# Strassen units of a fused FFN kernel in another order, with loads and sums at other places

## The chip, the cores and the metric

The kernel runs on one NeuronCore of a Trainium2 chip. The metric is the device time of one execution in microseconds; the median of several runs counts. One execution was also taken with the hardware profiler, and everything said of the inside of the kernel comes from that trace.

## The reference

Four layers are added to x (32 sequences, 64 channels, length 1024), each as a residual:

```python
x = x + s4_convolution(x, log_dt, C, log_A_real, A_imag, D, length)   # FFT convolution along L, masked
x = x + einsum('bsi,boi->bso', x, w1[ids1])                           # per-sequence 1024x1024 matrix
x = x + einsum('bij,bkj->bik', x, w2[ids2])                           # another one
gate = x @ W_gate.T + 0.5 * lora(x, A_gate, B_gate)                   # hidden size F = 2752, rank 16
up   = x @ W_up.T   + 0.5 * lora(x, A_up, B_up)
act  = silu(gate) * up
x = x + act @ W_down.T + 0.5 * lora(act, A_down, B_down)
```

All of it is fp32.

## The kernel before, in words

**Chunks.** The 32 sequences are cut into four chunks `c` of eight, so that a chunk has 512 columns. The convolution (L1037 on) runs first, for all sequences; chunk 0's result stays in SBUF, the results of chunks 1 to 3 go to the DRAM tensor `cd`. Then come chunk 0's 16 adapters (two layers of eight sequences, `adapter`, L287): each streams eight weight tiles of 512 KB through 128 matmul records into one PSUM bank `pa`. After that the feed-forward part `ffn` runs for chunk after chunk, and the 16 adapters of chunk c+1 are spread over the feed-forward part of chunk c as they come out of the generator `others`; `other(us)` (L851) first lets VectorE do postponed sums (`fill(us)`) and then runs one adapter.

**Blocks.** The hidden rows come in ten pairs, two pairs to a group `gi` (0 to 4), in three blocks: group 0; groups 1 and 2; groups 3 and 4. Of each group `gated` (L699) computes gate, then up. After a block, its part of the down product is added to x (`po<-act,wd` in the profile, 28 to 64 matmul records for each of four row blocks `h`). Rows that do not fit the Strassen scheme (`rest`, L730) are computed after block 0 with plain matmuls (`pr`); they are called the rest rows below.

**Strassen.** In chunk 0 gate and up use one level of the Winograd form of Strassen's scheme (`halves`), and the sums of weights are stored for later chunks on the way: `kept(q)` makes sums of sums and stores them in the DRAM tensors `sums` through two rotating buffers, `kept_parts` stores `parts`. Chunks 1 to 3 use two levels (`quarters`, L584): seven outer products, numbered 0 to 6 in the code and p1 to p7 as results, each made of the seven inner products P1 to P7 of `product(bank, i, start)`. One call of `quarters` makes gate or up of one group in 196 matmul records; there are 30 calls. Outer products are made one or two at a time by `unit(js, ...)`: before in the order (0), (5, 6), (4, 3), (1, 2). A unit with two has products of eight matmul records, a unit with one has products of four.

**Inside a unit.** Four PSUM banks `pa` to `pd` are used: P1 and P2 in `pa`, P6 in `pb`, P7 and then P4 in `pc`, P5 and then P3 in `pd`. ScalarE copies P1 and P6 out; VectorE makes u = P1 + P6 (L647), c22 = P7 + u (L649), c22 += P5 (L651), c21 = `pc` + u (L659), c12 = `pd` + u (L661). P4 is added by TensorE onto P7 in `pc`, and so has to wait until VectorE has read `pc` at L649; P3 is added onto P5 in `pd` and waits for L651.

**Order of the work.** TensorE, VectorE and ScalarE run in the order in which the code is written. The queues of SyncE (SP) and GpSimd (POOL) are ordered by the scheduler of the tile framework, and an SP load that waits for a buffer or a tile holds up those behind it. All weight tiles, `wa`, `wb`, `wd`, `wf`, `wr` and the convolution results `cv`, share a pool of nine buffers of 512 KB. Sums on VectorE that can wait are put into the deque `later` with an estimated cost each; `fill(us)` takes from its front while the estimates fit into `us`, `flush()` takes all.

**Places that the change touches.** `bring(c, quarters)` (L230) asks for x of the next chunk and for quarters of the convolution results, `take` (L246) puts the eight sums x += cv (two for each quarter) into `later`. Both are called by `between(i)` (L856), i = 2 gi after gate and 2 gi + 1 after up: quarters 0 and 1 after group 0's gate, 2 and 3 after block 0's first step of the rest rows. x has two buffers, so the request for the next x waits until the last chunk's rows in that buffer have been stored (`store`, L840). `between` runs no adapter for i = 2, `flush()` and one adapter for i = 3, and one adapter for i over 3; after the last group of blocks 1 and 2 there are a `flush()` and another adapter. `down_sides` (L879) loads and sums one tile of down weights; for the first tile of a block it is called through `behind`, after the last sum of up. `moving_act` makes the four sums of moving sides for one row pair of a group's activations, `times_up` the product of gate and up. `moving_of` makes the sides of the next chunk's x in four steps during the last down block.

Of the kernel before, what the change touches and what calls it, by code (L numbers as in the profile page):

```python
# [39 lines left out]
TH = TC // 2  # L40
# [33 lines left out]
def kernel(  # L74
# [25 lines left out]
    nc = tc.nc  # L100
# [27 lines left out]
    xs = [x_tile(0)]  # L128
# [101 lines left out]
    def bring(c, quarters):  # L230

        if quarters[0] == 0:
            xs.append(x_tile(c))
            with tc.issue_after(done_first[0]):
                nc.sync.dma_start(xs[c], xt[:, c])
        n = H // HA // 4
        for q in quarters:
# [8 lines left out]
    def take(c, quarters):  # L246
        n, half = H // 4, KT * BC // 2
        for q in quarters:
            t = came.pop(q)
            for i in (0, 1):  # L250

                def add(q=q, t=t, i=i):
                    rows_ = slice(i * half, (i + 1) * half)
                    xv = xs[c].rearrange("p k (b h) -> p (k b) h", h=H)
                    xv = xv[:, rows_, q * n : (q + 1) * n]
                    nc.vector.tensor_add(xv, xv, t.rearrange("p i k -> p k i")[:, rows_])

                later.append((1.0, add))
# [233 lines left out]
    def halves(c, gi, g, o, xb, sides0, behind, also=lambda: None):  # L492
# [37 lines left out]
        for m in range(MG):  # L530
# [27 lines left out]
            if m == 0:  # L558
                copy_lt()
                for at_, x in zip((wts, sts, sides_of), halves_sides(gi, g, 1)):  # L560
                    at_.append(x)
                kept_parts()
                also()
            else:
                fill(1.3)
            product(pc, 6, True)
            nc.vector.tensor_add(c22, pc, u)
            if m == 1:
                fill(1.3)
            product(pb, 4, True)  # L570
            nc.vector.tensor_add(c22, pb, c22)
            kept(2 * m)
# [4 lines left out]
            kept(2 * m + 1)  # L577
# [6 lines left out]
    def quarters(c, gi, g, o, xb, _, behind, also=lambda: None):  # L584
# [26 lines left out]
        def unit(js, start, mid, copies=None):  # L611
# [28 lines left out]
            fill(start)  # L640
# [8 lines left out]
            nc.vector.tensor_add(c22, pc, u)  # L649
            product(pd, 4, True)  # L650
            nc.vector.tensor_add(c22, pd, c22)  # L651
            if callable(mid):
                mid()
            else:
                fill(mid)
            product(pa, 1, False)
            nc.scalar.copy(c11, pa)
            product(pc, 3, False)
            nc.vector.tensor_add(c21, pc, u)  # L659
# [18 lines left out]
        (p1,) = unit((0,), 0.9, 0.0, copy_lt)  # L678
        nc.scalar.copy(c12, p1)
        also()  # L680
        add(c11, p1, l11)
        p6, p7 = unit((5, 6), 1.3, 1.3)
        add(c12, c12, p6)
        add(c21, c12, p7)

        def l12_():
            add(c12, c12, l12)
            fill(0.6)

        p5, p4 = unit((4, 3), 0.5, l12_)  # L690
        add(c22, c21, p5)
        add(c21, c21, p4)
        add(c12, c12, p5)
        p2, p3 = unit((1, 2), 0.0, lambda: add(o[:, 1], o[:, 1], lt[:, 1]))
        add(c11, c11, p2)
        add(c12, c12, p3)
        return behind()

    def gated(c, gi, xb, sides0, between, behind):  # L699


        f = quarters if c else halves
        act = apool.tile([P, 2, MG, TC], F32, tag="act", name=f"act_{c}_{gi}")
        sides0 = f(c, gi, 0, act, xb, sides0, lambda: c or halves_sides(gi, 1, 0))
# [14 lines left out]
        def moving_act(m):  # L719
            a = act[:, :, m]  # L720
            q = [a[:, h, t * TH : (t + 1) * TH] for h in (0, 1) for t in (0, 1)]
            ab.append(moving(*q, *(act_d[:, m, j] for j in range(4))))
# [3 lines left out]
        for m in range(MG):  # L726
            later.append((1.7, lambda m=m: moving_act(m)))
# [65 lines left out]
    def moving_of(c):  # L793
# [25 lines left out]
        def halves_of(i):  # L819
            b11, b12, b21, b22 = (q_of(k, t)[i] for k in (0, 1) for t in (0, 1))  # L820
            moving(b11, b12, b21, b22, *(at_(j)[i] for j in (4, 5, 6, 3)))
            for j, q in zip(range(3), (b11, b21, b22)):
# [6 lines left out]
            lambda: halves_of(1),  # L829
            lambda: (  # L830
                nc.vector.tensor_sub(t1, b12, b11),
# [14 lines left out]
    def ffn(c, xb, sides0, others):  # L846
# [24 lines left out]
        for block, (m0, m1) in enumerate(BLOCKS):  # L871
# [24 lines left out]
            for gi in groups:  # L896
                end = gi == groups[-1]

                def behind():
                    if end:  # L900
                        down_sides()
                    elif c == 0:
                        return halves_sides(gi + 1, 0, 0)

# [31 lines left out]
            if last:  # L936
# [3 lines left out]
                for t in (0, 1):  # L940
                    wl_t = wl[:, t].rearrange("p i f -> p (i f)")
                    gather(wl_t[FIRST], bd, rows_half[FIRST, c, t : t + 1])
                    with tc.issue_after(done_first[0]):
                        nc.sync.dma_start(wl_t[SECOND], wd_rest)
# [5 lines left out]
            for h in range(KH):  # L950
# [7 lines left out]
                for s0 in range(m0, m1, SEG):  # L958
# [6 lines left out]
                    elif end and last:  # L965
                        if h == 0:
                            nc.vector.tensor_sub(wl[:, 1, 0], wl[:, 1, 0], wl[:, 1, 1])
# [524 lines left out]
```

## Time and profile before

| what | us |
|---|---|
| runs before (three) | 2430.5, 2431.6, 2436.9 |
| median | 2431.6 |
| the profiled execution: time | 2439.8 |
| the profiled execution: span | 2438.2 |
| mean granted TensorE clock in it | 0.987 |
| DMA moved | 686 MB, mean 281 GB/s |

The span is the time from the first to the last instruction of the program in the profile, and the execution's time is 1.6 us more. PE is TensorE's matmuls, PEld its weight loads, DVE VectorE, ACT ScalarE, POOL GpSimd, SP SyncE, whose DMA issues are marked SPq. In a line of the page's list of groups, the first pair of numbers after the bar is the busy time of the group and the mean length of one instruction in ns, and what follows the second bar is the idle time of the engine before these instructions and what ended it. An fp32 matmul appears as two records.

### The profile page before, as it was taken

What the parts mean: (1) busy time and instruction counts of PE and PEld (TensorE: products, weight loads), DVE (VectorE), ACT (ScalarE), POOL (GpSimd) and SP (SyncE); (2) the same over time, 40 slices, a digit from 0 to 9 for tenths busy, and PEclk for the clock granted to TensorE, in tenths of its full rate; (3) what the DMA queues carried; (4) which work ended last, traced back from release to release, by engine and by line L of the source; (5) the groups of instructions that cost most, each with busy time, mean ns of one, the idle gap of its engine ahead of it and who ended that gap; (6) DMA issues with size and microseconds to landing.
All of it is one profiled execution on the core that took longest, in us unless ns stands there. A gap on an engine that the chain in (4) does not pass through costs nothing.

```text
span 2438.2 us, 53622 instructions
## 1 busy us (share of the span) xinstructions
PE 2293.7 (94%) x21674; PEld 1875.5 (77%) x21674; DVE 1321.0 (54%) x2762; ACT 386.6 (16%) x848; POOL 267.6 (11%) x387
## 2 busy tenths in 40 slices
PE   5999889999999898999999998999999899999998
PEld 4986447876667678798688688797688678798987
DVE  7411128775357555666345555666345556566574
ACT  4200012111001112131012112121012112121220
POOL 4322011211011210000000110100000110100000
PEclk9999999999999999999999999999999999999999
DMA  8999998489989856489989957489989957375581
GB/s 299 348 322 370 407 376 291 177 316 345 329 295 338 317 216 250 154 299 342 349 306 345 335 211 260 142 304 339 346 309 337 332 214 247 114 257 200 199 279 40
DMA packets 202121, 686.00 MB, mean 281 GB/s; under 512 B 26242, under 2 KB 28546, under 8 KB 201362
## 3 DMA queue, kind: packets, MB, share of 16 engines
q1 hardware_dynamic: 169890, 591.55, 67.1%
q0 software_dynamic: 25184, 82.37, 9.1%
q10 hardware_dynamic: 6800, 8.65, 1.0%
q8 instruction: 171, 2.80, 0.5%
q14 instruction: 76, 0.62, 0.1%
HBM read 615.07 MB, written 67.40 MB: 280 GB/s over the span
## 4 chain that ended last, share of the span: by engine, by line
PE 77%; DMA 18%; DVE 4%; issue 1%; ACT 0%; SPq 0%; DVEq 0%; POOL 0%; ACTq 0%
PE pq L620 25%; PE po L977 22%; DMA wa<-in_w 12%; PE pf L535 10%; PE pa L294 10%; PE pc L1280 4%; PE pr L746 3%; DMA wa<-sums 3%; DMA hk<-kp 1%; PE pe L423 1%; PE pl_d L394 1%; DMA x<-in_xt 1%; DMA kp<-ks 0%; DVE br L1082 0%; PE pl_u L394 0%
## 5 line engine op out<-in xcount | busy, mean ns | idle before, releaser
L294 PE MATMUL pa<-wa,x 128*32 128x256 f32 x7872 | 473.8, 385 | 63.5 <-DMA wa<-in_w 61.0
L294 PEld LDWEIGHTS pa<-wa,x 128*32 128x32 f32 x7872 | 239.0, 110 | 282.7 <-DMA wa<-in_w 123.1
L620 PE MATMUL pq<-xd,wa 128*128 128x128 f32 x3360 | 420.9, 277 | 6.6 <-DMA wa<-sums 6.5
L620 PEld LDWEIGHTS pq<-xd,wa 128*128 128x128 f32 x3360 | 398.9, 193 | 9.5 <-DMA wa<-sums 6.4
L620 PE MATMUL pq<-xd,wb 128*128 128x128 f32 x2520 | 334.6, 280 | 19.7 <-DVE t L649 18.9
L620 PEld LDWEIGHTS pq<-xd,wb 128*128 128x128 f32 x2520 | 307.7, 194 | 26.8 <-DVE t L649 22.4
L304 DVE STREAM_TRANSPOSE y<-pa 128x512 f32<-128x512 f32 x64 | 45.9, 716 | 328.0 <-PE pa L294 327.8
L977 PE MATMUL po<-actd,s 128*128 128x256 f32 x640 | 167.5, 385 | 5.4 <-DVE actd L464 3.5
L977 PE MATMUL po<-act,wd 128*128 128x256 f32 x640 | 170.8, 390 | 0.0
L1280 PE MATMUL pc<-uf,hk 128*128 128x256 f32 (+7 forms) x1024 | 154.7, 313 | 15.9 <-DMA hk<-kp 9.8
L322 POOL DMA_INDIRECT bgu<-in_bgu,rows x44 | 50.9, 1157 | 1052.1 <-PE pe L423 889.4
L1280 PEld LDWEIGHTS pc<-uf,hk 128*128 128x128 f32 x1024 | 149.4, 196 | 20.5 <-issue 13.3
L977 PE MATMUL po<-actd,wd 128*128 128x256 f32 x640 | 165.1, 381 | 0.0
L535 PE MATMUL pf<-xd,wf 128*128 128x256 f32 x640 | 151.9, 383 | 0.0
L449 DVE TENSOR_TENSOR s<-wd 128x256 f32<-128x256 f32 x80 | 33.9, 424 | 214.0 <-PE po L977 208.1
L977 PEld LDWEIGHTS po<-act,wd 128*128 128x128 f32 x640 | 118.8, 191 | 31.6 <-issue 16.6
L977 PEld LDWEIGHTS po<-actd,s 128*128 128x128 f32 x640 | 123.4, 193 | 24.0 <-DVE actd L464 4.7
L535 PEld LDWEIGHTS pf<-xd,wf 128*128 128x128 f32 x640 | 121.7, 192 | 17.7 <-issue 0.4
L977 PEld LDWEIGHTS po<-actd,wd 128*128 128x128 f32 x640 | 122.3, 191 | 16.9
L1003 ACT COPY uo<-po 128x256 f32<-128x256 f32 x48 | 17.9, 372 | 714.4 <-PE po L977 607.0
L535 PE MATMUL pf<-xd,s 128*128 128x256 f32 x480 | 113.5, 379 | 0.8 <-ACT u L554 0.5
L535 PEld LDWEIGHTS pf<-xd,s 128*128 128x128 f32 x480 | 91.0, 190 | 13.8 <-ACT u L554 0.8
(226 smaller groups left out, 2558.4 us busy)
## 6 DMA issues: line engine op xcount, KB each, us to landing
wa<-in_w SPq DMA_DIRECT2D x492, 512.0 KB, 7.7
wa<-sums SPq DMA_DIRECT2D x210, 512.0 KB, 5.6
wb<-parts SPq DMA_DIRECT2D x120, 384.0 KB, 5.0
wd<-in_wd SPq DMA_DIRECT2D x80, 512.0 KB, 6.6
wb<-in_wq SPq DMA_DIRECT2D x90, 384.0 KB, 5.9
hk<-kp SPq DMA_DIRECT2D x30, 1024.0 KB, 8.6
sums<-kept POOLq DMA_DIRECT2D x30, 1024.0 KB, 6.8
wf<-in_wg SPq DMA_DIRECT2D x20, 512.0 KB, 9.2
```

What stands on the lines that cost most here:

```text
L294: nc.tensor.matmul(acc[i * S : (i + 1) * S, s * 256 : (s + 1) * 256], xs[c][:, kt, lo + s * S : lo + (s + 1) * S], wt[:, i * 256 : (i + 1) ...
L304: nc.vector.transpose(y, acc)
L322: nc.gpsimd.indirect_dma_start(out=t, out_offset=None, in_=table, in_offset=bass.IndirectOffsetOnAxis(ap=at_, axis=0),)
L394: nc.tensor.matmul(ps[pair(j)], at[:, i, pair(j)], x_i[:, 2 * H * j : 2 * H * (j + 1)], start=(i == 0), stop=(i == n - 1),)
L423: nc.tensor.matmul(ps[:, at_ * 2 * H : (at_ + 1) * 2 * H], bt[pair(j), g], tms[table][pair(j)], start=(g == 0), stop=True, skip_group_chec ...
L449: nc.vector.tensor_add(s1, a21, a22)
L535: nc.tensor.matmul(ps, ws[j][:, kt, :], xb[j][:, kt, :], start=start and kt == 0, stop=kt == KH - 1, skip_group_check=True,)
L620: nc.tensor.matmul(ps[:, to * TQ : (to + 1) * TQ], w[i][:, k, :], xb[:, j, SLOT[i], k, :], start=start and k == 0 and to == 0, stop=k == K ...
L746: nc.tensor.matmul(ps, wts[i][:, kt, :], xs[c][:, kt, :], start=(kt == 0), stop=(kt == KT - 1),)
L977: nc.tensor.matmul(pss[j], *term, start=(s0 == m0 and i == 0 and home[j] % 2 == 0), stop=(end and i == len(terms) - 1), skip_group_check=True,
L1003: nc.scalar.copy(u1, p1)
L1280: nc.tensor.matmul(ps[:, j, d * B :], hk[:, j, d * P : (d + 1) * P], uf[:, i + j, : KT - d, :].rearrange("p k b -> p (k b)"), start=(d == ...
```

## The change

- **Units and banks.** `quarters` takes the outer products in the order (0, 5), (6, 4), (1, 3), (2). Inside a unit P4 goes to `pb`, with a start of its own, and VectorE makes c21 = P7 + u, c22 = P5 + c21, c21 += P4, c12 = `pd` + u. p1 is no longer copied by ScalarE. Postponed sums have places at the start of the first unit (2.5) and in the middle of the first (1.3); `early`, in the middle of the second, is what used to come behind the last sum, or a `fill(1.3)`.
- **Next x and convolution results.** `bring` and `take` are called once for all four quarters, at the rest rows after block 0.
- **Adapters.** `between` runs `other(5.0)` for every i from 1 on, so that block 1's first gate is followed by an adapter and there is no flush at i = 3; after the last group of block 2 there is no adapter.
- **Other sums.** In `halves`, kept(2) comes ahead of P7's sum, kept(3) after P5's. `moving_act` postpones its four sums as two pieces of 0.85 in place of one of 1.7. One sum of `moving_of` goes to an earlier step. `wd_rest` is loaded once, and ScalarE copies it to its second place.

```diff
-    def bring(c, quarters):
-        if quarters[0] == 0:
-            xs.append(x_tile(c))
-            with tc.issue_after(done_first[0]):
-                nc.sync.dma_start(xs[c], xt[:, c])
+    def bring(c):
+        xs.append(x_tile(c))
+        with tc.issue_after(done_first[0]):
+            nc.sync.dma_start(xs[c], xt[:, c])
...
             else:
-                fill(1.3)
+                kept(2)
             product(pc, 6, True)
             nc.vector.tensor_add(c22, pc, u)
-            if m == 1:
-                fill(1.3)
             product(pb, 4, True)
             nc.vector.tensor_add(c22, pb, c22)
-            kept(2 * m)
+            kept(3 * m)
...
-            kept(2 * m + 1)
+            if m == 0:
+                kept(1)
+            else:
+                fill(2.6)
...
-            fill(start)
+            if copies:
+                fill(2.5)
...
             product(pc, 6, True)
-            nc.vector.tensor_add(c22, pc, u)
+            nc.vector.tensor_add(c21, pc, u)
             product(pd, 4, True)
-            nc.vector.tensor_add(c22, pd, c22)
-            if callable(mid):
-                mid()
-            else:
-                fill(mid)
+            nc.vector.tensor_add(c22, pd, c21)
+            mid()
             product(pa, 1, False)
             nc.scalar.copy(c11, pa)
-            product(pc, 3, False)
-            nc.vector.tensor_add(c21, pc, u)
+            product(pb, 3, True)
+            nc.vector.tensor_add(c21, pb, c21)
             product(pd, 2, False)
             nc.vector.tensor_add(c12, pd, u)
...
-        (p1,) = unit((0,), 0.9, 0.0, copy_lt)
-        nc.scalar.copy(c12, p1)
+        p1, p6 = unit((0, 5), lambda: fill(1.3), copy_lt)
         also()
         add(c11, p1, l11)
-        p6, p7 = unit((5, 6), 1.3, 1.3)
-        add(c12, c12, p6)
+        add(c12, p1, p6)
+        p7, p5 = unit((6, 4), early)
         add(c21, c12, p7)
-
-        def l12_():
+        add(c22, c21, p5)
+        add(c12, c12, p5)
+
+        def rows1():
             add(c12, c12, l12)
-            fill(0.6)
-
-        p5, p4 = unit((4, 3), 0.5, l12_)
-        add(c22, c21, p5)
+            add(o[:, 1], o[:, 1], lt[:, 1])
+
+        p2, p4 = unit((1, 3), rows1)
+        add(c11, c11, p2)
         add(c21, c21, p4)
-        add(c12, c12, p5)
-        p2, p3 = unit((1, 2), 0.0, lambda: add(o[:, 1], o[:, 1], lt[:, 1]))
-        add(c11, c11, p2)
+        (p3,) = unit((2,), lambda: None)
         add(c12, c12, p3)
-        return behind()
...
+            later.append((0.85, lambda: (sub(t1, b12, b11), sub(t2, b22, t1))))
+            later.append((0.85, lambda: (sub(t3, b22, b12), sub(t4, b21, t2))))
...
         def between(i):
-            if i > 2:
-                if i == 3:
-                    flush()
+            if i:
                 other(5.0)
-            elif more_come and i < 2:
+            else:
                 store()
-                bring(c + 1, (2 * i, 2 * i + 1))
-                take(c + 1, (2 * i, 2 * i + 1))
...
                 if end:
                     flush()
-                    if block:
+                    if block == 1:
                         other()
...
                 next(left)
-                between(1)
+
+                if more_come:
+                    bring(c + 1)
+                    take(c + 1)
                 next(left)
                 flush()
```

More of the change, by code (lines that the diff above doesn't have):

```diff
@@ L228, in flush @@
             later.popleft()[1]()
-    def bring(c, quarters):
-        if quarters[0] == 0:
-            xs.append(x_tile(c))
-            with tc.issue_after(done_first[0]):
-                nc.sync.dma_start(xs[c], xt[:, c])
+    def bring(c):
+        xs.append(x_tile(c))
+        with tc.issue_after(done_first[0]):
+            nc.sync.dma_start(xs[c], xt[:, c])
         n = H // HA // 4
-        for q in quarters:
+        for q in range(4):
             t = wpool.tile([P, n * HA, KT * BC], F32, tag="w", name=f"cv{c}_{q}")
@@ L244, in bring, with take @@
             came[q] = t
-    def take(c, quarters):
+    def take(c):
         n, half = H // 4, KT * BC // 2
-        for q in quarters:
+        for q in range(4):
             t = came.pop(q)
@@ L582, in halves, with quarters @@
         return behind()
-    def quarters(c, gi, g, o, xb, _, behind, also=lambda: None):
+    def quarters(c, gi, g, o, xb, _, early, also=lambda: None):
         name = f"{c}_{gi}_{g}"
@@ L609, in load, with unit @@
             ]
-        def unit(js, start, mid, copies=None):
+        def unit(js, mid, copies=None):
             n = len(js)
@@ L677, in quarters @@
         l11, l12, _, _ = quarter(lt)
-        (p1,) = unit((0,), 0.9, 0.0, copy_lt)
-        nc.scalar.copy(c12, p1)
+        p1, p6 = unit((0, 5), lambda: fill(1.3), copy_lt)
         also()
         add(c11, p1, l11)
-        p6, p7 = unit((5, 6), 1.3, 1.3)
-        add(c12, c12, p6)
+        add(c12, p1, p6)
+        p7, p5 = unit((6, 4), early)
         add(c21, c12, p7)
-        def l12_():
+        add(c22, c21, p5)
+        add(c12, c12, p5)
+        def rows1():
             add(c12, c12, l12)
-            fill(0.6)
-        p5, p4 = unit((4, 3), 0.5, l12_)
-        add(c22, c21, p5)
+            add(o[:, 1], o[:, 1], lt[:, 1])
+        p2, p4 = unit((1, 3), rows1)
+        add(c11, c11, p2)
         add(c21, c21, p4)
-        add(c12, c12, p5)
-        p2, p3 = unit((1, 2), 0.0, lambda: add(o[:, 1], o[:, 1], lt[:, 1]))
-        add(c11, c11, p2)
+        (p3,) = unit((2,), lambda: None)
         add(c12, c12, p3)
-        return behind()
     def gated(c, gi, xb, sides0, between, behind):
         f = quarters if c else halves
+        if c:
+            first = lambda: fill(1.3)
+        else:
+            first = lambda: halves_sides(gi, 1, 0)
         act = apool.tile([P, 2, MG, TC], F32, tag="act", name=f"act_{c}_{gi}")
-        sides0 = f(c, gi, 0, act, xb, sides0, lambda: c or halves_sides(gi, 1, 0))
+        sides0 = f(c, gi, 0, act, xb, sides0, first)
         between(2 * gi)
@@ L720, in moving_act @@
             a = act[:, :, m]
-            q = [a[:, h, t * TH : (t + 1) * TH] for h in (0, 1) for t in (0, 1)]
-            ab.append(moving(*q, *(act_d[:, m, j] for j in range(4))))
+            b11, b12, b21, b22 = (a[:, h, t * TH : (t + 1) * TH] for h in (0, 1) for t in (0, 1))
+            t1, t2, t3, t4 = (act_d[:, m, j] for j in range(4))
+            ab.append((b11, b21, b22, t4, t1, t2, t3))
+            sub = nc.vector.tensor_sub
+            later.append((0.85, lambda: (sub(t1, b12, b11), sub(t2, b22, t1))))
+            later.append((0.85, lambda: (sub(t3, b22, b12), sub(t4, b21, t2))))
         for i in (0, 1):
@@ L726, in gated @@
         for m in range(MG):
-            later.append((1.7, lambda m=m: moving_act(m)))
+            moving_act(m)
         return act, ab, sides0
@@ L828, in moving_of @@
             lambda: halves_of(0),
-            lambda: halves_of(1),
+            lambda: (halves_of(1), nc.vector.tensor_sub(t1, b12, b11)),
             lambda: (
-                nc.vector.tensor_sub(t1, b12, b11),
                 nc.vector.tensor_sub(t2, b22, t1),
@@ L856, in between @@
         def between(i):
-            if i > 2:
-                if i == 3:
-                    flush()
+            if i:
                 other(5.0)
-            elif more_come and i < 2:
+            else:
                 store()
-                bring(c + 1, (2 * i, 2 * i + 1))
-                take(c + 1, (2 * i, 2 * i + 1))
         left = rest(c)
@@ L903, in behind @@
                         return halves_sides(gi + 1, 0, 0)
+                    else:
+                        fill(1.3)
                 act, ab_, sides0 = gated(c, gi, xb, sides0, between, behind)
@@ L942, in ffn @@
                     gather(wl_t[FIRST], bd, rows_half[FIRST, c, t : t + 1])
-                    with tc.issue_after(done_first[0]):
-                        nc.sync.dma_start(wl_t[SECOND], wd_rest)
+                with tc.issue_after(done_first[0]):
+                    nc.sync.dma_start(wl[SECOND, 0].rearrange("p i f -> p (i f)"), wd_rest)
                 if more_come:
@@ L966, in ffn @@
                         if h == 0:
+                            nc.scalar.copy(wl[SECOND, 1], wl[SECOND, 0])
                             nc.vector.tensor_sub(wl[:, 1, 0], wl[:, 1, 0], wl[:, 1, 1])
```

## The prediction

> **What bounds the kernel now.** I read the page first, then summed the trace by stage, because a share of 94% says nothing about where the rest is.
>
> ```profile
> span 2438.2 us, 53622 instructions
> ...
> PE 2293.7 (94%) x21674; PEld 1875.5 (77%) x21674; DVE 1321.0 (54%) x2762; ACT 386.6 (16%) x848; POOL 267.6 (11%) x387
> ...
> L294 PE MATMUL pa<-wa,x 128*32 128x256 f32 x7872 | 473.8, 385 | 63.5 <-DMA wa<-in_w 61.0
> ...
> L620 PE MATMUL pq<-xd,wb 128*128 128x128 f32 x2520 | 334.6, 280 | 19.7 <-DVE t L649 18.9
> ```
>
> TensorE is the bound, and its idle time has two addresses: the adapters (`pa`) wait for weights, and P4's products (`pq<-xd,wb`) wait for VectorE's line 649. The next view cuts the trace into the 30 calls of `quarters` (columns: stretch, length, PE busy and count, granted clock, DMA share, GB/s).
>
> ```profile
> 948.12:979.33 31.21, 25.37 (x196) 0.89 0.81 312
> 1035.15:1057.24 22.09, 22.09 (x196) 1.00 0.67 227
> ...
> 1289.56:1312.20 22.64, 22.40 (x196) 1.00 0.90 342
> ...
> 2018.43:2042.45 24.02, 22.34 (x196) 1.00 0.64 213
> ...
> 2168.47:2197.29 28.82, 24.51 (x196) 0.88 0.63 222
> ...
> sum 705.95, PE 680.11; mean PE 22.67
> ```
>
> The floor of a call is 22.08 us. Thirty would take 662.4, so 43.5 us are lost: 9.1 and 8.7 in chunk 1's and 2's second call, where next x arrives; 6.7 at 2168, where `flush` stands after group 1 of chunk 3; 1.9 in each chunk's first call; the rest in slips of 0.3 to 2. The timeline shows how the first kind happens.
>
> ```profile
> 950.71 0.33 SPq L235 DMA_DIRECT2D x<-in_xt  x1
> ...
> 957.39 0.37 ACT L657 COPY t<-pq 128x256 f32<-128x256 f32 x1 [2.35 <-PE pq L620]
> 960.17 1.05 DVE L256 TENSOR_TENSOR x<-x,cv 128x512 f32<-128x512 f32 x1 [7.48 <-DMA wb<-in_wq]
> 961.13 0.42 DVE L647 TENSOR_TENSOR u<-u,u 128x256 f32<-128x256 f32 x1
> 961.66 0.42 DVE L649 TENSOR_TENSOR t<-pq,u 128x256 f32<-128x256 f32 x1
> 962.13 2.08 PE L620 MATMUL pq<-xd,wb 128*128 128x128 f32 x8 [4.82 <-DVE t L649]
> ```
>
> (Columns: start, duration, engine, line, operation, out<-in, shapes, count, idle before and who ended it.) x is requested when its old contents have been stored, and lands at 960.05. A sum x += cv, put ahead of unit (5,6) by its `fill`, waits 7.48 us for it. Line 649, which must read bank `pc` before P4 may add into it, stands behind that. The wait costs twice: afterwards matmuls come every 213 ns instead of 113.
>
> ```profile
> 962.00:964.00 2.00, 1.87 (x8) 1.87 (x9) 1.44 (x3) 0.00 (x0) 0.00 (x0) 0.50 0.03 12
> ```
>
> (The clock is the third number from the end.) Last, the ends of block 2, chunk 1 (adapter, 28 down matmuls, adapter) and chunk 3 (28 matmuls):
>
> ```profile
> 1375.00:1388.75 13.75, 9.37 (x130) 4.00 (x129) 8.28 (x17) 0.00 (x0) 6.18 (x10) 0.84 1.01 288
> 1388.75:1396.22 7.47, 7.47 (x32) 6.15 (x28) 2.93 (x6) 0.00 (x0) 0.00 (x0) 0.83 1.03 303
> 1396.22:1405.62 9.40, 8.17 (x129) 3.48 (x132) 1.52 (x4) 0.00 (x0) 0.00 (x0) 1.00 1.02 407
> ...
> 2367.86:2380.60 12.74, 9.19 (x30) 6.60 (x28) 12.23 (x29) 0.00 (x0) 1.90 (x2) 0.73 0.82 206
> ```
>
> Undisturbed, an adapter takes 7.04 and 28 matmuls 6.24. DMA is full (share 1.0) at only 288 GB/s in the first row, since eight `raw_g` loads in short pieces run then; in chunk 0's adapters it moved 407.
>
> **What the Trainium skill says.** "TensorE: Matmul & The Clock Gate", Part 1 (What's actually happening): an array idle for about 3.4 us falls to half clock and needs about as long busy to recover. The trace agrees: after 4.82 us idle it shows 0.50 from 962 to 968, after 1.67 (first calls) it doesn't. Same page, Architectural detail: VectorE is strictly first in, first out; the 7.48 us above show it. "PSUM — Partial Sum Buffer", PSUM bank collisions raise a hardware error: guard PSUM by bank, not by address; hence the wait on line 649, and why a bank of its own removes it. "DMA: Bandwidth & Descriptors", Specifications: a ceiling of 435 GB/s; here 407 to 415 is the most seen.
>
> **The change, part by part.**
>
> *P4 in bank `pb`.* The same 196 matmuls and five VectorE operations a unit. P4 now needs only ScalarE's copy of P6, three products old. What can still hold TensorE is P3, which adds into `pd` after line 651's successor has read it. In a pair a product lasts 0.90 us. First unit of a chunk's first call: VectorE frees at 926.43 (timeline), three operations at 0.43 end it at 927.7; P3's turn is 923.0 + 6 x 0.90 = 928.4. So 1.9 x 3 vanish, and the slips of 0.36 in second calls too.
>
> *Lone P3 last.* Its products last 0.45. Before it, VectorE finishes the pair's last sum 0.62 us into the unit, then adds p2 and p4: in chunk 1's timeline such adds start 0.11 after it and go at 0.73 and 0.61 (973.80, 974.53, 975.14), so it is free at 2.07. Three small operations go every 0.39 (926.43, 926.82, 927.21): the third ends at 3.14, the matmul follows 0.05 later (962.08 to 962.13): 3.19. P3's turn is 6 x 0.45 = 2.70. So each call gains a new stall of 0.49, x 30 = 15 us. Bounds: 0 if these adds overlap more, 1 if `rows1` (1.8 us) pushes the pair's sum by half a microsecond. I take 0.5.
>
> *x and cv at the rest rows.* SP's order in the built program has x's request behind P7 and P5's weights of chunk 1's second call and ahead of the next four; the cv loads follow wr. No sum waits for it there: 17.9 go. But x (2.1 MB) still starts after the stores, about 950, and P2 and P4's four loads (1.8 MB) queue behind it: 3.9 MB at 0.415 MB/us is 9.4 us, landing near 961 against a need at 959 to 960: 1.7 us remain twice (0 to 5). Eight cv sums of 1.04 now stand in the flush: in chunk 1 it ended at 993.8 and rest's sums began at 996.0; four more sums less the down sides, made earlier (1.5), end it at 996.5: free. In chunk 0 there is no such slack (flush to 421.7, first use of `rest1` at 425.8, `wm` at 429.7): about 1 us.
>
> *Down sides inside unit (6,4), `fill` of 2.5, 1.3, 1.3.* The sides (four operations, 1.45 us) stand between the sums of P5 and P4, where VectorE has 1.4 us free; behind them waits P4's sum, which no matmul of the unit needs. Their `wd` is requested a call ahead; if it were late, the next unit's P3 would wait. A `fill` of 2.5 after an adapter ends 0.8 us after the unit's first sum could start, which is made up before P5 is there (3.6 us); the sum that P3 waits for ends at 4.2, its turn is 5.4. Both cost nothing.
>
> *All calls.* After: 15 + 3.4 + 6 of DMA waits as now (6.5 in the list of waits) = 24.4, against 43.5; the flush at group 1 is gone. **19 us gained.**
>
> *An adapter moves from block 2's end to block 1's first gate.* Now lost at the end: chunk 1 6.71 + 1.23 + 2.36 = 10.3; chunk 2 11.2; chunk 0 (837.82 to 859.22) 4.4 + 3.7 = 8.1; together 29.6. After, one adapter remains behind 28 matmuls; its 4.2 MB and two `wd` loads of 0.5 at the first row's 288 GB/s take 18 us, while lone P3, 28 matmuls and the adapter itself give 3.2 + 6.2 + 7.0 = 16.4: 1.7 late, and the raw pieces may go on for longer; I take 2.5 in chunks 1 and 2 and 1.5 in chunk 0. In block 1 it costs 2.6 in chunk 0 (like the 9.66 us at 506) and 0.4 in chunks 1 and 2. 29.6 - 6.5 - 3.4: **20 gained** (bounds 0 and 26). The flush it covered has the 28 matmuls, which read group 3 alone.
>
> *Chunk 3's ends.* 8.25 and 12.74 against 6.24: 8.5 lost, since 1.7 us pieces fitted in no `fill` (1.3 at most) and down sides came last. Pieces of 0.85 fit, sides come inside unit (6,4): **8 gained.**
>
> *`kept` earlier (chunk 0).* kept(2) moves ahead of P7's sum and needs kept(0)'s buffer, stored 6.6 to 8.4 us after its issue (mean of seven, 7.2). From that issue: buffer free at 7.2, four sums 2.7, P7's and P5's sums to 10.9; P4's turn (second in its bank) is 9.95: 0.94 us a call. Seven calls are followed by an adapter that waits 2.6 for DMA anyway and gives it back; three are not: -3 (0 to -12). With the rest rows **-4**.
>
> *One `wd_rest` load and a ScalarE copy (some 1 us), one t1 sum in another step, no copy of p1 on ScalarE:* nothing, ScalarE is busy 16%.
>
> Sum: 19 + 20 + 8 - 4 = 43. Against the profiled execution's own 2439.8 (span 2438.2 and 1.6 around it) 2397; it was 8.2 above the median of the runs, 2431.6, from which I take it: **2389**.
>
> **Rivals.** (a) *Lone P3 costs nothing and no DMA wait remains at block 2's end*: 15 + 6.5 more, 2367. For: VectorE is busy 54%. Against: the sum above. (b) *The adapter's wait only moves*: four in block 1 run at 342 GB/s beside calls, seven more follow; 20 is lost, 2409. For: DMA shares of 0.9. Against: adapters inside block 2 took 7.4. (c) *The change doesn't take x out of the way*: the four loads behind it land as late as 963 did, with half clock after: 14 back, 2403. (d) *Slower: lone P3 with `rows1`*. If the pair's last sum waits behind `rows1` fully, 1.9 more fall on each of 30 ends: 57 - 43 makes 14 slower, 2446; it decides from 1.4 us a call. Against: between the sums of P5 and P4 VectorE has 1.4 us free and `rows1` needs 1.8, so only 0.4 is passed on, and P3's product, which comes after, hides that.
>
> **Numbers.** Forecast 0.50, (a) 0.18, (b) 0.13, (c) 0.09, (b), (c) and `kept` at its worst together 0.03 (2431, no change), (d) 0.07. Range 2368 to 2412: (a)'s lower half, (d) and the joint case fall out. By 0.3%, what can be told from no change: faster 0.90, same 0.03, slower 0.07.
>
> **What would show it.** Calls of 22.5 with the idle time on P3 behind line 653; no half clock in chunks 1 to 3 before the last block; adapters within 2 us of 7.04 at block 2's ends; chunk 0 about even. Wrong: calls above 23.5, x's sums at the head of VectorE's waits, or adapters of 10 us in block 1 of chunks 1 and 2.

## The result, and the profile after

The changed kernel took 2392.8 us as the median of four runs (2388.0 to 2393.7), beside 2434.3 for the kernel before, also of four: a ratio of 0.9825, 95% interval 0.9801 to 0.9849, or some 42 us. The forecast was 2389. The total came out; of the four terms under it only one, chunk 3's ends, came out close, as the experiments below show.

The page of the changed kernel (same columns as before: busy time and mean ns, then the idle time before these instructions and its releaser):

```profile
span 2390.6 us, 53647 instructions
...
PE 2277.6 (95%) x21674; PEld 1869.2 (78%) x21674; DVE 1314.9 (55%) x2762; ACT 379.7 (16%) x822; POOL 266.3 (11%) x387
...
L293 PE MATMUL pa<-wa,x 128*32 128x256 f32 x7872 | 466.5, 382 | 41.4 <-DMA wa<-in_w 39.2
L621 PE MATMUL pq<-xd,wa 128*128 128x128 f32 x3360 | 423.5, 277 | 15.8 <-DMA wa<-sums 8.2
...
L621 PE MATMUL pq<-xd,wb 128*128 128x128 f32 x2520 | 325.4, 277 | 5.2 <-DMA wb<-in_wq 5.2
```

Set beside the lines of before: adapters wait 39.2 us for weights in place of 61.0. P4's line no longer waits for VectorE at all; its 18.9 us are gone. In their place `pq<-xd,wb` waits 5.2 us for a transfer, and `pq<-xd,wa` has 15.8 us, 7.0 of it on VectorE's line 653 and 8.2 on DMA.

I cut both traces where the kind of matmul changes and added the stretches up (a stretch lasts to the start of the next one):

| stretches | before, us | after, us | difference |
|---|---|---|---|
| convolution (not touched) | 179.0 | 173.7 | -5.3 |
| 10 gate and up calls of chunk 0 | 246.2 | 250.7 | +4.5 |
| 48 adapters among the feed-forward parts | 399.9 | 373.3 | -26.6 |
| 30 calls of `quarters` | 706.0 | 700.7 | -5.3 |
| down products | 570.9 | 558.4 | -12.5 |
| the rest | 336.2 | 334.6 | -1.6 |
| span | 2438.2 | 2390.6 | -47.6 |

The first row is a warning. Nothing in the convolution differs between the kernels, and it took 170 to 180 us in the 14 profiles of this study. So spans of single profiles are not compared below; stages are, and the medians of the runs.

The calls of `quarters`, after (stretch, length, PE busy and count, granted clock, DMA share, GB/s):

```profile
909.03:931.60 22.57, 22.34 (x196) 1.00 0.68 229
932.71:959.39 26.68, 23.28 (x196) 1.00 0.92 347
...
1110.85:1134.74 23.89, 22.80 (x196) 1.00 0.91 333
...
1468.26:1497.48 29.22, 25.61 (x196) 0.88 0.83 318
...
2256.80:2279.38 22.58, 22.35 (x196) 1.00 0.81 288
...
sum 700.63, PE 679.51; mean PE 22.65
```

There are three sorts. An undisturbed call, such as most of chunk 3's, is 22.57 or 22.58: the old floor of 22.08 and exactly the 0.49 forecast for the lone P3. The two calls behind which next x is fetched are 26.68 and 29.22, better than 31.2 and 30.8, but not the 24.3 that was forecast. And the calls of chunks 1 and 2 that stand between adapters are 23.2 to 24.3, at a DMA share of about 0.9.

The timeline shows the lone P3 (start, duration, engine, line, operation, names, shapes, count, idle before and who ended it):

```profile
1266.09 0.69 DVE L691 TENSOR_TENSOR act<-act,t 128x512 f32<-128x512 f32 x1
...
1266.70 0.68 DVE L692 TENSOR_TENSOR act<-act,t 128x512 f32<-128x512 f32 x1
...
1267.30 0.28 DVE L649 TENSOR_TENSOR u<-u,u 128x128 f32<-128x128 f32 x1
...
1268.09 0.29 DVE L653 TENSOR_TENSOR t<-pq,t 128x128 f32<-128x128 f32 x1
...
1268.43 0.71 PE L621 MATMUL pq<-xd,wa 128*128 128x128 f32 x4 [0.23 <-DVE t L653]
```

The two adds of p2 and p4 (lines 691 and 692) stand ahead of the three small sums, and line 653, for which P3 waits, ends at 1268.38. (The bracket says 0.23 and not 0.49, since idle time is counted from an end of the matmuls before that the profile models; the lengths of the calls give the 0.49.)

The ends of block 2 in chunks 1 and 2 and of chunk 3's blocks (PE, PEld, DVE, ACT and POOL busy, clock, DMA share, GB/s):

```profile
1363.36:1369.49 6.13, 6.13 (x30) 5.13 (x28) 5.92 (x12) 2.32 (x3) 3.16 (x6) 1.00 1.03 288
1369.49:1380.27 10.78, 7.76 (x129) 3.71 (x132) 3.35 (x10) 0.00 (x0) 1.22 (x3) 1.00 1.02 377
...
1910.76:1922.21 11.45, 9.04 (x129) 4.01 (x132) 3.34 (x10) 0.00 (x0) 1.16 (x3) 0.85 1.03 368
...
2326.64:2332.78 6.14, 6.14 (x30) 5.14 (x29) 5.93 (x12) 1.57 (x2) 0.00 (x0) 1.00 1.05 262
```

Here the 28 down matmuls are at their floor, chunk 3's too; in chunk 0, which is not shown, they take 8.53. The adapter behind them is not at its floor: 3.7 and 4.4 us late, with DMA full, and in chunk 2 partly at half clock (0.85).

### The profile page after: what moved, and what is told of

Same layout as the page of the kernel before. It is cut to its first block, busy times and chain, and to the rows that moved or that the text cites. A ratio compares the mean times of both kernels' runs of the same rounds, so it can differ in the third digit from the quotient of the medians.

```text
span 2390.6 us, 53647 instructions
## 1 busy us (share of the span) xinstructions
PE 2277.6 (95%) x21674; PEld 1869.2 (78%) x21674; DVE 1314.9 (55%) x2762; ACT 379.7 (16%) x822; POOL 266.3 (11%) x387
## 4 chain that ended last, share of the span: by engine, by line
PE 66%; DMA 15%; issue 11%; DVE 6%; POOL 1%; POOLq 0%; ACT 0%; DVEq 0%; SPq 0%; ACTq 0%
PE pq L621 24%; PE po L982 22%; PE pa L293 8%; PE pc L1285 5%; DMA wa<-sums 4%; DMA wa<-in_w 3%; PE pr L751 3%; DMA sums<-kept 2%; PE pf L534 2%; DMA wf<-in_wu 1%; DMA wf<-in_wg 1%; DMA hk<-kp 1%; PE pe L422 1%; PE pl_d L393 1%; POOL parts L524 0%
## 5 line engine op out<-in xcount | busy, mean ns | idle before, releaser
L293 PE MATMUL pa<-wa,x 128*32 128x256 f32 x7872 | 466.5, 382 | 41.4 <-DMA wa<-in_w 39.2
L621 PE MATMUL pq<-xd,wa 128*128 128x128 f32 x3360 | 423.5, 277 | 15.8 <-DMA wa<-sums 8.2
L293 PEld LDWEIGHTS pa<-wa,x 128*32 128x32 f32 x7872 | 244.2, 110 | 248.0 <-DMA wa<-in_w 91.1
L621 PEld LDWEIGHTS pq<-xd,wa 128*128 128x128 f32 x3360 | 396.7, 192 | 26.1 <-DVE t L653 12.5
L621 PE MATMUL pq<-xd,wb 128*128 128x128 f32 x2520 | 325.4, 277 | 5.2 <-DMA wb<-in_wq 5.2
L621 PEld LDWEIGHTS pq<-xd,wb 128*128 128x128 f32 x2520 | 301.5, 192 | 9.6 <-DMA wb<-in_wq 5.8
L1285 PE MATMUL pc<-uf,hk 128*128 128x256 f32 (+7 forms) x1024 | 154.4, 313 | 10.9 <-DMA hk<-kp 5.4
L982 PEld LDWEIGHTS po<-act,wd 128*128 128x128 f32 x640 | 118.3, 191 | 29.8 <-issue 14.7
```

Of the source, the lines that this page charges most:

```text
L293: nc.tensor.matmul(acc[i * S : (i + 1) * S, s * 256 : (s + 1) * 256], xs[c][:, kt, lo + s * S : lo + (s + 1) * S], wt[:, i * 256 : (i + 1) ...
L621: nc.tensor.matmul(ps[:, to * TQ : (to + 1) * TQ], w[i][:, k, :], xb[:, j, SLOT[i], k, :], start=start and k == 0 and to == 0, stop=k == K ...
L982: nc.tensor.matmul(pss[j], *term, start=(s0 == m0 and i == 0 and home[j] % 2 == 0), stop=(end and i == len(terms) - 1), skip_group_check=True,
L1285: nc.tensor.matmul(ps[:, j, d * B :], hk[:, j, d * P : (d + 1) * P], uf[:, i + j, : KT - d, :].rearrange("p k b -> p (k b)"), start=(d == ...
```

## The experiments

Times are ratios to the kernel before, run on the same chip in the same session. The first three take one part of the change alone, on the kernel before.

**The order of units alone** (`e1_units`): the new `quarters` in the old kernel, x and the adapters left in place.

```diff
-        (p1,) = unit((0,), 0.9, 0.0, copy_lt)
+        p1, p6 = unit((0, 5), lambda: fill(1.3), copy_lt)
...
-            product(pc, 3, False)
-            nc.vector.tensor_add(c21, pc, u)
+            product(pb, 3, True)
+            nc.vector.tensor_add(c21, pb, c21)
```

> The kernel before with the changed `quarters` alone (order of the outer products, P4 in `pb`, places of the postponed sums, `early`); loads, adapters and chunk 0 as before. My theory: the slips of 0.3 us behind line 649 and the 1.9 us of each chunk's first call go (about 12 us), the flush of chunk 3 hurts less (about 5 us), but a lone P3 waits 0.49 us in each of 30 calls (15 us more), and x's sums still stop VectorE in chunks 1 and 2. Together -3 us (-10 to +5), and every undisturbed call at 22.57 us. Rival: the units' order is what the whole change lives on: -25 us or more.

Measured 0.9990 (0.9981 to 0.9999), 2.4 us. Undisturbed calls are 22.57, but the two calls behind x grow to 39.3 and 38.7; there TensorE waits for VectorE's line 653, 12.8 us at the longest, while the sums of x still stand ahead of it. (The profiled execution, 2447.5 us, was the slowest of 22 with a median of 2436.3, so these two lengths may be high.)

```profile
PE pq L621 <- DVE t L653: 31.8, 33, 12.8
```

(Total in us, times, longest.) This run also holds most of what the change wins at chunk 3's ends, because the down sides stand inside unit (6, 4) here too: the two ends take 6.14 and 7.09 us in place of 8.25 and 12.74. So the new order by itself is worth next to nothing; it trades one stall for another.

**x and the convolution results alone** (`e2_x`):

```diff
-            elif more_come and i < 2:
+            elif i == 0:
                 store()
-                bring(c + 1, (2 * i, 2 * i + 1))
-                take(c + 1, (2 * i, 2 * i + 1))
...
                 next(left)
-                between(1)
+                if more_come:
+                    bring(c + 1)
+                    take(c + 1)
```

> The kernel before with the request for x, the loads of convolution results and their sums moved to the rest rows, all else as before. My theory: the second calls of chunks 1 and 2, 31.2 and 30.8 us before, fall to about 25 us, because x still lands while the next weights are needed: -10 us (-15 to -6). Rival: the load itself is the cost wherever its sums stand: calls stay above 28 us and the time within 4 us of before.

Measured 0.9966 (0.9949 to 0.9983), 8.3 us, about what was expected; the two calls behind x come to 26.8 and 24.1.

**The adapter alone** (`e3_adapters`):

```diff
-            if i > 2:
+            if i > 1:
...
-                    if block:
+                    if block == 1:
                         other()
```

> The kernel before with the one adapter moved from behind block 2 to behind block 1's first gate (the flush behind block 1's first group kept), all else as before. My theory: the ends of block 2 get faster by about 23 us over three chunks, the extra adapter in block 1 costs about 3: -20 us (-26 to -12). Rival: the wait for adapter weights only moves into block 1, where adapters then take 9 us or more in chunks 1 and 2: within 5 us of before.

Measured 0.9944 (0.9922 to 0.9966), 13.7 us (8 to 19), at the low end of what was expected. In its profile chunk 1's and 2's adapters take 123.4 and 124.2 us (129.2 and 130.2 before), but chunk 0's, 145.3 in place of 140.6, show no gain; in `e1_units` and `e2_x`, which leave the adapters where they were, they take 144.4 and 139.3.

**The changed kernel with `halves` as before** (`e4_kept`), to see what the earlier kept(2) and kept(3) cost:

```diff
-                kept(2)
+                fill(1.3)
             product(pc, 6, True)
...
-            kept(3 * m)
+            kept(2 * m)
...
```

> The changed kernel with `halves` as before (kept(2) and kept(3) at their old places, two fills of 1.3). My theory: calls of gate and up in chunk 0 go back from 25.1 to about 24.6 us, since nothing waits for the `kept` buffers: -4 us (-7 to 0) against the changed kernel, about 2389. Rival: the earlier stores are why chunk 0's adapters got shorter (7.6 to 9.6 us after the change, 9.6 to 11.1 before); then these go back to 9.6 and more and the time is 6 us or more above the changed kernel.

Measured 0.9861 (0.9838 to 0.9884): some 9 us *slower* than the changed kernel (about 1 to 17 by the two intervals together). My sign was wrong. The cost that I had seen is there, chunk 0's gate and up calls fall from 250.7 to 247.1 us; but its 16 adapters rise from 130.1 to 144.5. That is no accident of one execution: they take 126.6 to 130.9 in the six profiles of full-size kernels with the early kept, and 139.3 to 145.3 in the five without. The six adapters that follow a gate or up call are where it happens. First this kernel, then the changed one; matmuls of the adapters alone (stretch, length, PE busy and count, clock, DMA share, GB/s):

```profile
481.99:491.83 9.84, 7.45 (x128) 1.00 1.00 339
...
sum 62.33, PE 46.47; mean PE 7.75
```

```profile
477.30:485.06 7.76, 7.25 (x128) 1.00 1.03 379
...
sum 50.39, PE 44.48; mean PE 7.41
```

and around the first of the six the issues of the kept sums' stores in the timeline, in the same order:

```profile
480.17 0.72 POOL L511 DMA_DIRECT2D sums<-kept  x1 [7.92 <-DVE kept L451]
...
482.56 0.56 POOL L511 DMA_DIRECT2D sums<-kept  x1 [1.67 <-DVE kept L451]
```

```profile
473.03 0.72 POOL L511 DMA_DIRECT2D sums<-kept  x1 [5.76 <-DVE kept L451]
...
477.89 0.56 POOL L511 DMA_DIRECT2D sums<-kept  x1 [4.13 <-DVE kept L451]
```

(The adapter begins at 481.99 in the first and at 477.30 in the second.) With kept late, 1.5 MB of stores are issued within 2 us of the adapter's start and share the DMA engines with its weights. With kept early the larger store leaves 4.3 us ahead of it. That is a reading of two traces; a run below tests it.

**The lone P3's stall removed** (`e5_p3`): the two adds go into the middle of the lone unit.

```diff
         p2, p4 = unit((1, 3), rows1)
-        add(c11, c11, p2)
-        add(c21, c21, p4)
-        (p3,) = unit((2,), lambda: None)
+        (p3,) = unit((2,), lambda: (add(c11, c11, p2), add(c21, c21, p4)))
         add(c12, c12, p3)
```

> The changed kernel with one edit: in each call of quarters the adds c11 += p2 and c21 += p4 stand in the middle of the lone unit (2), after VectorE's sum over its P5, and no longer ahead of that unit's first sum. The lone unit's t has a buffer of its own, so that p2 and p4 stay readable. My theory: the 0.49 us stall of the lone P3 behind line 653 comes from these two adds, which hold the queue of VectorE; without them an undisturbed call takes 22.08 to 22.15 instead of 22.57. 30 calls x 0.49 = 14.7 is the most; calls beside adapters that wait for DMA may give part of it back, so 8 to 14 us faster than the changed kernel: about 2379 to 2385 where that one gives 2393. Rival: the calls of chunks 1 and 2 are limited by the transfers of their own and the adapters' weights, and TensorE's stall only hides that; then only chunk 3's 10 calls gain, 5 us or less.

Measured 0.9809 (0.9792 to 0.9826). That is 4 us below the changed kernel, give or take 7, and the same edit on top of the next run's (`e7_both` beside `e6_xlate`) brings 3: less than the 8 to 14 expected, and by the time the rival. Yet the stall is gone: undisturbed calls take 22.09. All calls together fall by only 6.8 us, of which 4.8 are chunk 3's ten, that have no adapters between them; the two calls behind x rise by 3.4, and the adapters by 6.2. In this profile the time moved from one wait into another.

**x behind the weights of the rest rows** (`e6_xlate`):

```diff
-        with tc.issue_after(done_first[0]):
+        with tc.issue_after(last_wr[0]):
             nc.sync.dma_start(xs[c], xt[:, c])
...
-            nc.sync.dma_start(wt.rearrange("p k f -> p (k f)"), wr[i])
+            last_wr[:] = [nc.sync.dma_start(wt.rearrange("p k f -> p (k f)"), wr[i]).ins]
...
```

> The changed kernel with one edit: the request for next x waits until the last wr load of the rest rows has been issued, so that SP has it behind both wr and ahead of cv, and no longer ahead of the four weight loads of the second call's unit (1, 3). My theory: what the second calls of chunks 1 and 2 still lose (26.68 and 29.22 against 22.57: 4.1 and 6.65 us) is the time for which these four loads stand behind 2.1 MB of x; with x later these calls take 22.6 to 23, and 8 to 11 us go, less 1 to 2 for x's sums, which come later at the rest rows. Rival: the same transfer then holds up wd or the next block's first weights or the first sums of the rest rows, and the loss reappears within 20 us of its old place: 0 to 3 us.

Measured 0.9803 (0.9786 to 0.9819): again little in the total, 5 us, give or take 7. The two calls behind x take 22.48 and 22.92, so the cause of their loss was named rightly, and all calls fall by 10.9 us. But chunk 0's gate and up calls rise by 10.2, 9.0 of it in one call:

```profile
351.13:384.64 33.51, 26.77 (x112) 0.90 0.75 273
```

The timeline says why:

```profile
362.10 0.42 SPq L234 DMA_DIRECT2D x<-in_xt  x1
...
365.05 0.72 POOL L511 DMA_DIRECT2D sums<-kept  x1 [2.38 <-DVE kept L451]
...
375.32 0.69 DVE L448 TENSOR_TENSOR kept<-s 128x512 f32<-128x512 f32 x1 [7.46 <-DMA sums<-kept]
```

In chunk 0 x now falls onto the stores of kept, and kept(2) waits 7.46 us for its buffer at the head of VectorE's queue. In the changed kernel x had been requested at 338.59 there, and the same kept(2) waited 0.62.

**Both** (`e7_both`):

> The changed kernel with both edits: the adds of p2 and p4 in the middle of the lone unit, and next x requested behind the last wr load. If the two losses are separate, the gains add: 18 to 24 us below the changed kernel, 2369 to 2375 where it gives 2393. If the weights of the calls in chunks 1 and 2 set the pace, part is given back: 10 us or less.

Measured 0.9789 (0.9767 to 0.9810), about 9 us below the changed kernel, half of the 18 to 24 expected. Calls fall by 19.5 us, chunk 0's calls rise by 8.4 and adapters by 6.4.

**P4's bank without the new order** (`e8_order`):

```diff
+        (p1,) = unit((0,), lambda: None, copy_lt)
+        nc.scalar.copy(c12, p1)
...
+        p6, p7 = unit((5, 6), lambda: fill(1.3))
...
+        p5, p4 = unit((4, 3), early)
...
+        p2, p3 = unit((1, 2), rows1)
```

> The changed kernel with the outer products in the order of the kernel before, (0), (5, 6), (4, 3), (1, 2), p1 copied by ScalarE again, and P4 still in bank pb with a start of its own. This tells the bank of P4 from the order. My theory: the bank alone takes away the stall of P4 in the lone first unit and costs nothing; with the lone unit first, its P3 meets no adds of VectorE, so an undisturbed call takes 22.08 to 22.2 and 8 to 14 us go against the changed kernel. Rival: the lone unit's P3 stalls wherever it stands, since its products are too short (0.45 us) for VectorE's three sums: calls stay at 22.5 and the time is within 3 us of the changed kernel's.

Measured 0.9828 (0.9810 to 0.9845), the same as the changed kernel: by the time, the rival, and not the 8 to 14 us of my theory. The calls look different all the same: 22.1 to 22.5 where nothing disturbs them, but 24.0 to 24.3 in each chunk's first call, where postponed sums ahead of the lone unit hold P3 for 1.6 to 1.9 us at line 653. Calls come to 695.5 us and adapters to 382.6. P4's own bank is as good in the old order; order and bank are separate questions.

**x late only in chunks 1 and 2** (`e9_late12`): both edits, but chunk 0 asks for x where the changed kernel does.

```diff
-        with tc.issue_after(last_wr[0]):
+        with tc.issue_after(last_wr[0] if c > 1 else done_first[0]):
```

> The version with both edits (adds of p2 and p4 inside the lone unit, next x behind the last wr load), but the request of x for chunk 1, made in chunk 0, stays where the changed kernel has it. With x moved in chunk 0 too, chunk 0's gate and up calls took 259 to 261 us in place of 250.7, because x's 2.1 MB shared the DMA engines with the stores of kept (365.05 to 378.98 in place of some 7 us), for which kept(2) waits. My theory: that loss of 8 to 10 us goes and the gain in chunks 1 and 2 stays: 6 to 10 us below the version with both edits, ratio to the kernel before about 0.975. Rival: chunk 0's loss has another cause (the sums on VectorE, or the profile's one execution): the same ratio as with both edits, 0.979.

Measured 0.9761 (0.9737 to 0.9785), 2378.2 us beside 2436.0: the fastest full version of the study, some 15 us below the changed kernel (7 to 24 by the two intervals together). Chunk 0's calls are at 252.5 again and all calls of `quarters` at 684.1. The next three show what still holds those calls and the adapters.

**Half of the adapters' transfers** (`l1_light` and `l2_light_p3`), on the changed kernel and on `e5_p3`:

```diff
-                if k in held:
+                if kt % 2 and b >= BC:
+                    yield wt
+                elif k in held:
                     yield held.pop(k)
```

> The changed kernel, in which the adapters of chunks 1 to 3 load only four of their eight weight tiles and use each twice: 2.1 MB instead of 4.2 per adapter, the same 128 matmul records. The output is another one. If what the calls and adapters of chunks 1 and 2 lose above 22.57 and 7.04 is a wait for transfers, the 20 calls but the two behind x come down to 22.57 and 47 of the 48 adapters that stand among the feed-forward parts to 7.04 to 7.3 where they belong to chunks 1 to 3: 18 calls x about 0.9 of loss = 12 to 15 us, adapters 373 to about 341: 30 us; 35 to 45 us below the changed kernel. Rival: these losses come from VectorE or ScalarE: less than 10 us.

> The version with the adds of p2 and p4 inside the lone unit, with the same lighter adapters (four of eight weight tiles loaded, each used twice; the output is another one). In full size that edit took 6.8 us from the calls in the profile and 6.2 came back in the adapters. My theory: it came back because the DMA engines are full in chunks 1 and 2 (share 0.91 to 0.93 from 1110 to 1400), so with lighter adapters the edit brings its full 12 to 15 us: this kernel 11 to 15 us below the lighter changed kernel. Rival: what came back is not a matter of transfers (matmuls at a lower clock, noise between two executions): 3 to 7 us as in full size.

Measured 0.9649 (0.9634 to 0.9665) and 0.9586 (0.9570 to 0.9603); the medians are 2350.4 and 2335.6. The first is some 43 us below the changed kernel: the same matmuls, half the bytes, and the waits go. Its calls, then those of the second:

```profile
918.38:947.38 29.00, 25.65 (x196) 0.88 0.84 317
1003.21:1025.78 22.57, 22.34 (x196) 1.00 0.69 234
1033.93:1056.50 22.57, 22.34 (x196) 1.00 0.79 277
```

```profile
916.72:946.60 29.88, 25.69 (x196) 0.89 0.82 309
1002.42:1024.51 22.09, 22.09 (x196) 1.00 0.67 238
1032.66:1054.75 22.09, 22.09 (x196) 1.00 0.76 270
```

DMA share is 0.8 in place of 0.9, calls among adapters take the undisturbed 22.57 and 22.09, and all 48 adapters take 6.93 or 7.04 (337.4 us together) in both. The call behind x is not helped, since its wait is for x and not for adapters. Between the medians of the two kernels lie 14.8 us, give or take 6, where the stalls removed are 30 x 0.49 = 14.7; in the two profiles the calls fall by 10.4, since the two behind x and a few others give some back. The edit that was worth 3 or 4 us in full size is worth most or all of its 14.7 here, and no adapter gets longer. So what came back in `e5_p3` came back as waits for weights.

Which property of the lighter adapters does it is not settled. They move half the bytes, and they also take half as many of the pool's nine buffers, so that the loads behind them can be issued sooner. That the DMA engines are full at such a wait can be seen in the changed kernel: in the call at 1648.84, where TensorE waits twice for `wa` for 0.51 us at 1650.2 and 1651.4, the share is 1.02 and 1.03 from 1646 to 1654. No run gives the adapters fewer buffers or fewer bytes alone.

**`halves` as before, with light adapters** (`l3_light_kept`):

> The changed kernel with kept(2) and kept(3) at their old places in halves (as in the run e4) and with the lighter adapters (four of eight weight tiles loaded, each used twice; the output is another one). In full size the old places cost 8.8 us against the changed kernel: its adapters took 14.2 us more and its gate and up calls of chunk 0 3.6 less. My theory: the earlier kept is a gain only because its stores leave before the next adapter's weights are read; where adapters no longer fill the DMA engines, what is left is VectorE's wait for the buffer, and the sign turns: the old places are 2 to 5 us faster than the lighter changed kernel (ratio 0.9649), so about 0.963 to 0.964, with the 48 adapters still at 7.04 to 7.2. Rival: the gain of the earlier kept has nothing to do with the adapters' weights: this kernel stays 6 to 10 us slower than the lighter changed one, 0.967 to 0.969.

Measured 0.9604 (0.9584 to 0.9623), 11 us *faster* than the lighter changed kernel (give or take 6), where in full size the same edit was 9 us slower. The sign turns, by more than I had put it. Chunk 0's calls are 244.1 us (ten at the 24.37 of the shortest would be 243.7) in place of 249.5, and the adapters stay at 337.4 with both; the rest of the 11 us is within what these runs scatter. The earlier kept is a cost to TensorE's own work that pays only through the adapters' weights.

## Why the prediction was right, and where it was not

*P4 in bank `pb`; the lone P3.* Right: no wait on P4, 22.57 a call. Also right that the postponed sums cost nothing there. The prediction puts the wait on line 649 down to the rule on PSUM banks that it takes from the Trainium skill. The code alone calls for it: P4 is added onto the values of P7 that this line reads. A bank of its own takes both reasons away, and no run here tells them apart.

*x and cv at the rest rows: "1.7 us remain twice".* The mechanism was right, four weight loads queue behind x; the term was mis-sized: 4.1 and 6.65 in this profile. Chunk 2's call is the dearer since its wait of 3.24 us is followed by half clock. `e6_xlate` takes nearly the whole of it away. In the five other profiles with the same order of units that fetch x at the same place (`e4_kept`, `e5_p3` and the three light ones) the two calls take 27.7 to 30.8, so that 4.1 is the lucky end.

*"6 of DMA waits as now".* Wrong in size, and the step of the calls' sum that failed: the other calls lose 12.8 us (700.7 less 30 x 22.57, less 10.75 in the two calls behind x). With light adapters this goes (`l1_light`), so it is waits for weights. The calls lose 14.7 + 10.8 + 12.8 = 38.3 against 43.5 before, so **5 gained in place of 19** in the profile. I had carried over a wait from a kernel in which other stalls gave DMA time to catch up; `e5_p3` and `l2_light_p3` fit this reading.

*An adapter moves: 20.* By itself 13.7. The forecast had 6.5 left at block 2's ends; in the changed kernel they lose 3.7 (chunk 0), 4.3 (with 0.5 of the next adapter) and 4.4, 12.4 in all. I reckoned 18 us of transfers against 16.4 of work. Why the weights come later than that is not shown: DMA was not behind at the start (share 0.76 from 1358 to 1362 in chunk 1), but it is full from 1366 to 1380, and from 1371.49 on the next loads are issued while this adapter still waits for its last tiles.

*Chunk 3's ends: 8.* Right, 8.25 + 12.74 became 6.14 + 6.14, 8.7 us; 7.8 of it is already in `e1_units`. The parts that were measured alone sum to 2.4 + 8.3 + 13.7 + 8.8 = 33. The other 9 of the 42 belong to no part by itself. A likely share is that the new order made the two calls behind x longer while the sums of x stood in them, a loss that goes when x moves; no run has just these two parts together.

*`kept` earlier and the rest rows: -4.* The cost of 3 was sized well: 3.6 in the calls, and the 0.65 us wait on `wm` in chunk 0 is there. The sign of the whole was wrong. I followed kept(2) to the product that waits for it, and noted that seven of ten calls are followed by an adapter that waits for DMA and "gives it back"; I did not ask what the store's new time does to that adapter. It is 14 us in the profiles, and by the runs the step gains some 9.

So 14 less than forecast in the calls and 6 less in the adapters met 13 more in `kept` and about 5 that these terms don't account for, which is within the scatter of the runs. That the total came out is luck: errors of both signs, as large as a third of the gain, cancelled.

The signs named beforehand say the same. Calls of 22.5 with P3 behind line 653 came. Half clock was not to come in chunks 1 to 3 before the last block, and did, in chunk 2's second call; the adapters at block 2's ends were to be within 2 us of 7.04 and were 3.7 and 4.4 late; chunk 0 was not even (calls 4.5 longer, adapters 10.5 shorter). And nine calls besides the two behind x took more than 23.5, which was named as a sign of being wrong.

The rivals: (a) falls, the stall of the lone P3 is in every call and 12.4 us remain at block 2's ends; but removing that stall is worth 3 or 4 us in full size, not 15. (b) falls in the main: of the 20, 6 are missing, at block 2's ends and not in block 1, where no adapter of chunks 1 and 2 takes more than 9.0. (c) came half true: the two calls behind x lose 10.8 in place of 3.4, 7 of its 14. (d) falls: the pair's last sum (line 660) waits for TensorE and not for `rows1`.

## What to carry to other kernels

Before a stall of an engine is priced as time to be won, look at the DMA share of the same stretch: at the 0.9 of this kernel a stall of TensorE was also the time in which loads caught up, and most of what was taken from it came back as the next wait for weights; halving the loads in a version that computes something else shows in one run how much. A store on another queue can compete with the next loads: ask of a moved step when its store now leaves, not only what its result holds up. And when a request is moved for a chunk in the middle, look at the first chunk on its own, where other transfers stand around it.

## What the runs showed of the hardware

The wait of 3.24 us in the changed kernel's second call behind x was followed by half clock (timeline, then windows, whose third number from the end is the clock):

```profile
1484.28 2.21 PE L621 MATMUL pq<-xd,wb 128*128 128x128 f32 x8 [3.24 <-DMA wb<-in_wq]
```

```profile
1481.04:1483.19 2.15, 0.00 (x0) 0.00 (x0) 1.98 (x4) 0.00 (x0) 0.00 (x0) 1.00 0.90 358
1483.19:1490.02 6.83, 5.60 (x22) 5.00 (x23) 0.85 (x2) 0.74 (x2) 0.00 (x0) 0.50 1.03 416
```

The clock fell 2.15 us into the wait and stayed at half for 6.83 us. So the wait of 3.24 cost some 6 us in all, twice what the list of waits says.

The four shorter waits of chunk 1's call (1.73 the longest) left it at 1.00. But that is no safe length. In `e9_late12` one wait of 1.83 us did this:

```profile
1305.08 1.26 PE L621 MATMUL pq<-xd,wa 128*128 128x128 f32 x6 [1.83 <-DMA wa<-sums]
```

```profile
1305.53:1308.94 3.41, 3.41 (x19) 3.41 (x18) 0.85 (x2) 2.33 (x5) 0.00 (x0) 0.50 0.84 325
```

and the trace of the kernel before has 0.50 from 53.26 to 56.67, in the convolution, after a wait of 1.67 us, the very length that the prediction calls harmless. So equal waits are followed by half clock at one place and not at another, and it lasts 3.41 us here and 6.83 there. "TensorE: Matmul & The Clock Gate" of the Trainium skill, Part 1, puts the drop at about 3.4 us idle; these traces have it after half of that too. The prediction takes the time to recover to be about as long; here it was up to 6.83.

The prediction calls 407 to 415 GB/s the most seen. In stretches of some length it is; the window 952 to 954 of the kernel before shows 467, at a DMA share of 1.16, and a share above 1 says how rough so short a window is.
